# Cross attention of a decoder on one Trainium2 core: half of the score tiles through VectorE with mask and adj added from PSUM, half through ScalarE and GpSimd, and layer norms cut into pieces

## The chip, the cores and the metric

The kernel runs on one core of a Trainium2 chip. A core has five engines that run their own instruction streams and wait for each other by semaphores: TensorE (PE; its weight loads are listed apart as PEld), VectorE (DVE), ScalarE (ACT), GpSimd (POOL) and SyncE (SP), which here issues most DMA transfers. Operands lie in SBUF (128 partitions); matmul results go to PSUM. The metric is the device time of one execution in microseconds; less is better.

## The reference, cut to what matters

The program is a decoder: self-attention, cross attention, two layers of local attention with a feed-forward part, a quantized attention, an attention over media, and a mixture of experts. The stages run one after the other on the same 8 × 512 × 256 array x. The change lies in the cross attention, of B = 8 batches, 512 queries, 512 keys and 16 heads of width 16, all in fp32:

```python
Q = heads(query, Wq, bq)
K = heads(key, Wk, bk)
V = heads(value, Wv, bv)
scores = jnp.einsum('bhqd,bhkd->bhqk', Q, K) / jnp.sqrt(jnp.float32(D))
scores = scores + adj[None, None, :, :]
scores = jnp.where(mask == 0, jnp.float32(-jnp.inf), scores)
weights = jax.nn.softmax(scores, axis=-1)
out = jnp.einsum('bhqk,bhkd->bhqd', weights, V)
out = out.transpose(0, 2, 1, 3).reshape(b, s, E)
return jnp.einsum('bse,ef->bsf', out, Wo.T) + bo
```

A layer norm stands ahead of it (over x, for the queries) and another behind it (for the next stage). The result is added to x.

## The kernel before

**Steps.** The stage is `stage_cross_attention`. Its main loop has 128 steps, 16 for each batch: four groups of four heads (g, e), and for each group four tiles of 128 keys (kt). Scores are held transposed, keys on the partitions and queries along the row, so no maximum over a row is taken; the softmax's sum comes from a column of ones beside the values.

In each step `scores` (L1640) runs four matmuls, one for each head of the group, on four row groups of the array, into two PSUM tiles `sc` of 128 × 2 × 512, two heads in each; three such tiles exist. `soften` (L1657) takes each of the two tiles through ScalarE's exponential into SBUF (`x_e`, six buffers, L1663), and VectorE multiplies it there by `x_share` (L1664), which is exp(adj) where the mask is set and zero elsewhere. `weigh` (L1669) runs two steps behind: four matmuls of the softened tiles with the values, added up over the four key tiles in one PSUM bank `po`.

**After a group.** ScalarE copies `po` to `x_o` (L1685), four DMAs sort its rows into `x_oT` (L1693), the sums go through DRAM into a compact layout, VectorE inverts them (L3174), they come back spread over rows as `x_wide` (L1703), and GpSimd multiplies `x_oT` by `x_wide` (L1696). When both halves of a batch are there, `project_out` (L1709) multiplies by the output weights, VectorE adds the result to x (L1717), the rows are sent to DRAM (`away`, L1720), and the layer norm of the next stage (`lt_ln`) is done on VectorE: statistics, three Newton steps for the inverse root (`rsqrt`, L1460 to L1464, on 128 × 4 elements) and four normalizations (L157).

**Preparing the next batch.** While a batch's steps run, the generator `prepare(b + 1)` gives out pieces of the next batch's preparation: loads (the context, and the mask of 1 MB into `x_mask`, a tile of its own), the layer norm `x_ln`, then `bias` added to x by GpSimd (L1570), two key projections (bias added by VectorE, L1601), four value projections (copied by ScalarE), four pieces of `x_share` (L1560, VectorE, from mask and adj, 128 × 512 each), two transposes and two query projections. All projections, transposes and `project_out` use one PSUM bank, `pj`. `x_share`, keys and queries have one tile for even and one for odd batches.

**What sets the order.** A list `later` of thunks with due steps holds the late parts (inverting, spreading, multiplying, `project_out`), at most two a step. `together` keeps a group's four matmuls adjacent. The framework then schedules the instructions of each engine and adds the waits; within an engine the resulting order is fixed, so an instruction that waits holds up all behind it on that engine. From the twelfth step before the end, the preparation of local attention is mixed in (`ahead.step(3)`), whose rotary embedding is VectorE work.

Of the kernel before, what the change touches and what calls it, by code (L numbers as in the profile page):

```python
# [27 lines left out]
F32 = mybir.dt.float32  # L28
# [11 lines left out]
P = 128  # L40
# [1237 lines left out]
class FastDecoder(Decoder):  # L1278
# [12 lines left out]
    NOWHERE = 8192.0  # L1291

    def __init__(self, ctx, tc, t):
        super().__init__(ctx, tc, t)
        self.sums = self.alloc(self.dram, [self.N_SUMS, 4, S], F32, "sums")
        self.invs = self.alloc(self.dram, [self.N_SUMS, 4, S], F32, "invs")
        self.n_sums = 0
# [158 lines left out]
    def rsqrt(self, pool, out, v, tag):  # L1456
# [4 lines left out]
        for _ in range(3):  # L1461
            nc.vector.scalar_tensor_tensor(t, out, -0.5, out, ALU.mult, ALU.mult)
            nc.vector.tensor_tensor(t, t, v, ALU.mult)
            nc.vector.scalar_tensor_tensor(out, t, 1.5, out, ALU.add, ALU.mult)  # L1464

    def load_cross_attention(self):
        w = self.weights()
        names = "x_wqT", "x_wkT", "b_wvT", "b_woT"
        return [self.load_w(w, 512 * i, self.t[n]) for i, n in enumerate(names)]
# [6 lines left out]
    def stage_cross_attention(self, ahead):  # L1476
# [40 lines left out]
        nc.vector.tensor_tensor(self.ok, self.ok, top, ALU.min)  # L1517
        nc.scalar.activation(adj, adj, AF.Exp)
        for e in range(2):
# [20 lines left out]
        def prepare(b):  # L1540
# [4 lines left out]
            def load():  # L1545
                d["ctxT"] = self.alloc(first, [P, 2, S], F32, "x_ctxT")
                nc.sync.dma_start(
                    d["ctxT"], t["ctxT"].rearrange("(k p) n -> p k n", p=P)[:, :, b * S : (b + 1) * S]
                )
                d["mask"] = self.alloc(first, [P, NST, S], I32, "x_mask", bufs=1)  # L1550
                nc.sync.dma_start(d["mask"], t["x_maskT"][b].rearrange("(k p) q -> p k q", p=P))
                nc.sync.dma_start(
                    self.slots[b * CAP : (b + 1) * CAP, :].rearrange("(p r) c -> p r c", p=P),
                    empty.unsqueeze(1).broadcast_to([P, CAP // P, self.WIDE]),
                )

            def share(k):
                if k == 0:
                    d["share"] = self.alloc(own, [P, NST, S], F32, f"x_share{b % 2}", bufs=1)
                nc.vector.scalar_tensor_tensor(  # L1560
                    d["share"][:, k, :], d["mask"][:, k, :], 0.0, adj[:, k, :], ALU.not_equal, ALU.mult
                )

            def norm():
                x = self.x[:, b * NST : (b + 1) * NST, :]
                stats = self.ln_stats(first, lambda i: [x[:, i, :]], NST, "x_ln")
                d["xn"] = self.alloc(first, [P, NST, C], F32, "x_xn", bufs=1)
                for i in range(NST):
                    self.normalize(d["xn"][:, i, :], x[:, i, :], stats, i)
                nc.gpsimd.tensor_tensor(x, x, bias.unsqueeze(1).broadcast_to([P, NST, C]), ALU.add)  # L1570
                d["xnT"] = self.alloc(first, [P, 2, S], F32, "x_xnT", bufs=1)
# [41 lines left out]

            yield load
            yield norm
            for g in range(2):
                yield lambda g=g: keys(g)
            for i in range(NST):
                yield lambda i=i: values(i)
                yield lambda i=i: share(i)  # L1620
            for c in range(2):
                yield lambda c=c: turn(c)
            for g in range(2):
                yield lambda g=g: queries(g)

        second = None
        for thunk in prepare(0):
            thunk()
            yield
        yield Ahead.MAIN  # L1630

        with self.tc.tile_pool(reuse_waits="tile", name="xa", bufs=2) as pool, self.tc.tile_pool(
# [7 lines left out]
            def scores(n):  # L1640
# [3 lines left out]
                d = held[b]  # L1644
                d.setdefault("e", {})[rest] = pair = []
                for p in range(2):
                    pair.append(self.alloc(psum, [P, 2, 512], F32, "sc", bufs=3))

                for m in self.together(4):
                    r = (m + 2) % 4  # L1650
                    rows = slice(32 * r, 32 * r + 32)
                    nc.tensor.matmul(  # L1652
                        pair[r // 2][:, r % 2, :], d["k"][rows, g, kt * P : (kt + 1) * P], d["q"][rows, e, g, :],
                        start=True, stop=True,
                    )

            def soften(n):  # L1657
                b, rest = divmod(n, 16)
                kt = rest % 4
                d = held[b]  # L1660
                for p in range(2):
                    ex = self.alloc(pool, [P, 2, 512], F32, "x_e", bufs=6)
                    nc.scalar.activation(ex, d["e"][rest][p], AF.Exp)  # L1663
                    nc.vector.tensor_tensor(  # L1664
                        ex, ex, d["share"][:, kt, :].unsqueeze(1).broadcast_to([P, 2, 512]), ALU.mult
                    )
                    d["e"][rest][p] = ex

            def weigh(n):  # L1669
# [7 lines left out]
                for m in self.together(4):  # L1677
                    r = (m + 2) % 4
                    nc.tensor.matmul(  # L1679
                        d["po"][32 * r : 32 * r + 32, :], d["v"][:, kt, 8 * g + 2 * r + e, :],  # L1680
                        ex[r // 2][:, r % 2, :], start=(kt == 0), stop=(kt == 3),
                    )
                if kt == 3:
                    o = self.alloc(pool, [P, S], F32, "x_o", bufs=3)
                    nc.scalar.copy(o, d["po"])  # L1685

                    if e == 0:
                        d["oT", g] = self.alloc(pool, [P, S], F32, "x_oT", bufs=5)
                        d["wide", g] = self.alloc(pool, [P, S], F32, "x_wide")
# [19 lines left out]
            def project_out(b, i):  # L1709
# [6 lines left out]
                x = self.x[:, b * NST + i, :]  # L1716
                nc.vector.tensor_tensor(x, x, ps[:, :C], ALU.add)  # L1717
                if i == NST - 1:
                    rows = self.x[:, b * NST : (b + 1) * NST, :]
                    nc.sync.dma_start(self.away[b], rows)  # L1720
                    stats = self.ln_stats(pool, lambda i: [rows[:, i, :]], NST, "lt_ln")
                    for i in range(NST):
                        self.normalize(rows[:, i, :], rows[:, i, :], stats, i)

            n = 16 * B
            ready = None
            for i in range(n + 2):
                if i < n:
                    if i % 16 == 0:
                        for thunk in ready or ():  # L1730
                            thunk()
                        ready = prepare(i // 16 + 1) if i // 16 + 1 < B else iter(())
                    scores(i)
                    soften(i)
                if i >= 2:
                    weigh(i - 2)

                for _ in range((0, 2, 2, 1, 2, 1, 2)[i % 16] if i % 16 < 7 else 1):
                    thunk = next(ready, None)
                    if thunk is not None:  # L1740
                        thunk()
                later.tick(2)
# [16 lines left out]
    def local_attention(self, l, y, ahead):  # L1759
# [64 lines left out]
        def rotate(d, i):  # L1824
# [13 lines left out]
            q4 = qk.rearrange("p (j h d) -> p j h d", j=2, d=64)  # L1838
            r = self.alloc(first, [P, 2 * S], F32, "la_r")
            r4 = r.rearrange("p (j h d) -> p j h d", j=2, d=64)  # L1840
# [1604 lines left out]
```

## Time and profile before

| | |
|---|---|
| time, median of 3 runs | 3174.21 us (3169.55 to 3178.64) |
| the profiled execution | 3162.05 us |
| its span in the trace | 3160.1 us, mean granted TensorE clock 0.973 |
| cross attention, first score to last weighted sum | 203.4 to about 711 us |
| of these 508 us busy: TensorE / VectorE / ScalarE / GpSimd | 428.4 / 426.4 / 309.2 / 44.8 us |
| mask of 1 MB: issue, landing after issue | 0.4 us, 4.6 to 5.9 us |

A line of the costliest groups gives the line of the code, the engine, the operation, output and inputs by their names in the program, shapes and count; behind the first bar the busy time in all and the mean of one in ns; behind the second the idle time just before them and what ended it. A line of the windows gives a stretch, its length, and busy time and instructions of each engine (PE, PEld, DVE, ACT, POOL), then the granted clock and the share of DMA. A line of the waits reads "who waited <- for what: total us, times, longest". A line of the timeline gives start, length, engine and instruction; in square brackets stands how long its engine had been waiting, and for what.

### The profile page before, as it was taken

What the parts mean: (1) busy time and instruction counts of PE and PEld (TensorE: products, weight loads), DVE (VectorE), ACT (ScalarE), POOL (GpSimd) and SP (SyncE); (2) the same over time, 40 slices, a digit from 0 to 9 for tenths busy, and PEclk for the clock granted to TensorE, in tenths of its full rate; (3) what the DMA queues carried; (4) which work ended last, traced back from release to release, by engine and by line L of the source; (5) the groups of instructions that cost most, each with busy time, mean ns of one, the idle gap of its engine ahead of it and who ended that gap; (6) DMA issues with size and microseconds to landing.
All of it is one profiled execution on the core that took longest, in us unless ns stands there. A gap on an engine that the chain in (4) does not pass through costs nothing. (4 is left out here: it accounts for less than half of the span.)

```text
span 3160.1 us, 40243 instructions
## 1 busy us (share of the span) xinstructions
PE 2877.0 (91%) x14929; PEld 1485.8 (47%) x14944; DVE 2166.9 (69%) x4962; ACT 1154.0 (37%) x1607; POOL 408.7 (13%) x389
## 2 busy tenths in 40 slices
PE   8998888877998989999988989998796999997998
PEld 5642222224555556655555546654444233333665
DVE  7458888887788795357788798558787766566110
ACT  2146556653434431123434431113353444342111
POOL 1111000000011010000101111111201122222111
PEclk9999999989999999999999999999997999998999
DMA  7011111111000001001000011001332122213331
GB/s 237 1 53 44 54 57 48 32 24 51 16 21 22 19 27 42 0 1 35 22 15 21 22 44 61 15 12 60 95 127 94 41 79 103 75 64 103 102 138 59
DMA packets 130695, 168.73 MB, mean 53 GB/s; under 512 B 51760, under 2 KB 79665, under 8 KB 128442
## 3 DMA queue, kind: packets, MB, share of 16 engines
q1 hardware_dynamic: 126394, 154.48, 15.6%
q0 software_dynamic: 4096, 11.59, 1.0%
q8 instruction: 119, 1.95, 0.3%
q14 instruction: 86, 0.70, 0.1%
HBM read 113.12 MB, written 47.50 MB: 51 GB/s over the span
## 5 line engine op out<-in xcount | busy, mean ns | idle before, releaser
L1812 PE MATMUL pj<-w,la_hT 128*128 128x512 f32 x720 | 345.3, 612 | 23.9 <-DVE la_v L1817 21.9
L1664 DVE TENSOR_TENSOR x_e<-x_e,x_share 128x1024 f32<-128x1024 f32 x256 | 309.1, 1253 | 25.1 <-ACT x_e L1663 24.3
L1663 ACT ACTIVATE x_e<-sc 128x1024 f32<-128x1024 f32 x256 | 249.7, 1026 | 147.9 <-PE sc L1652 145.5
L2817 ACT ACTIVATE ma_e<-sc,ma_bias 128x1024 f32<-128x1024 f32 x128 | 142.4, 1114 | 198.8 <-PE sc L2812 185.5
L1812 PEld LDWEIGHTS pj<-w,la_hT 128*128 128x128 f32 x720 | 129.5, 191 | 167.0 <-issue 119.0
L3188 POOL TENSOR_TENSOR la_oT<-la_o,x_wide 128x512 f32<-128x512 f32 x64 | 96.8, 1523 | 790.6 <-DMA x_wide<-invs 654.6
L2825 DVE TENSOR_TENSOR ma_esum<-ma_esum,ma_e 128x1024 f32<-128x1024 f32 x96 | 122.8, 1280 | 91.6 <-ACT ma_e L2817 90.9
L1933 ACT ACTIVATE la_e<-la_e 128x1024 f32<-128x1024 f32 (+1 forms) x128 | 121.4, 951 | 175.2 <-DVE la_e L1929 175.2
L2146 ACT ACTIVATE lf_gate<-pj,lf_b 128x512 f32<-128x512 f32 (+1 forms) x82 | 56.3, 687 | 338.1 <-PE pj L2125 327.1
L1679 PE MATMUL po<-x_e,x_v 128*32 128x512 f32 x1024 | 140.1, 620 | 37.2 <-DVE x_e L1664 34.1
L2125 PE MATMUL pj<-lf_hnT,w 128*128 128x512 f32 (+1 forms) x368 | 171.9, 595 | 1.2 <-DVE lf_hid L2151 1.1
L1929 DVE TENSOR_TENSOR la_e<-sc,la_mask 128x1024 f32<-128x1024 f32 (+1 forms) x128 | 138.3, 1081 | 38.8 <-PE sc L1922 38.8
L1652 PE MATMUL sc<-x_q,x_k 32*128 32x512 f32 x1024 | 159.2, 662 | 0.3 <-ACT x_e L1663 0.2
L2125 PE MATMUL sc<-lf_hnT,w 128*128 128x512 f32 x336 | 158.0, 592 | 0.0
L2197 PE MATMUL po<-w,lf_hid 128*128 128x256 f32 x640 | 148.9, 379 | 0.2 <-DVE x L2207 0.2
L1988 PE MATMUL pj<-w,la_oT 128*128 128x256 f32 x512 | 124.4, 389 | 23.4 <-ACT la_qkT L1858 12.6
L2812 PE MATMUL sc<-ma_qT,ma_kT 64*128 64x512 f32 x512 | 145.2, 644 | 0.0
L2151 DVE SCALAR_TENSOR_TENSOR lf_hid<-sc,lf_b,lf_gate 128x512 f32<-128x512 f32 x70 | 52.4, 748 | 126.3 <-PE sc L2125 126.3
L2835 PE MATMUL po<-ma_e,ma_v 128*64 128x512 f32 x512 | 138.1, 618 | 0.0
L1940 PE MATMUL po<-la_e,la_v 128*64 128x256 f32 (+1 forms) x1024 | 129.1, 374 | 6.4 <-ACT la_o L1962 6.3
L1922 PE MATMUL sc<-la_qkT 64*128 64x256 f32 (+1 forms) x1024 | 132.6, 378 | 1.3 <-DVE la_e L1929 1.3
L1819 ACT ACTIVATE la_sq<-pj 128x512 f32<-128x512 f32 x120 | 71.4, 595 | 156.2 <-PE pj L1812 155.9
(491 smaller groups left out, 5264.5 us busy)
## 6 DMA issues: line engine op xcount, KB each, us to landing
x_wide<-invs SPq DMA_DIRECT2D x184, 128.0 KB
w<-in_f_w_dram SPq DMA_DIRECT2D x16, 1024.0 KB
kv<-kv_o SPq DMA_DIRECT2D x56, 256.0 KB
slots<-x_empty SPq DMA_DIRECT2D x8, 1028.0 KB
x_mask<-in_x_maskT_dram SPq DMA_DIRECT2D x8, 1024.0 KB
ma_kT<-kv SPq DMA_DIRECT2D x8, 1024.0 KB
ma_v<-kv SPq DMA_DIRECT2D x8, 1024.0 KB
ex_rows<-slots SPq DMA_DIRECT2D x7, 1028.0 KB
```

The source lines that it names most:

```text
L1652: nc.tensor.matmul(pair[r // 2][:, r % 2, :], d["k"][rows, g, kt * P : (kt + 1) * P], d["q"][rows, e, g, :], start=True, stop=True,)
L1663: nc.scalar.activation(ex, d["e"][rest][p], AF.Exp)
L1664: nc.vector.tensor_tensor(ex, ex, d["share"][:, kt, :].unsqueeze(1).broadcast_to([P, 2, 512]), ALU.mult)
L1679: nc.tensor.matmul(d["po"][32 * r : 32 * r + 32, :], d["v"][:, kt, 8 * g + 2 * r + e, :], ex[r // 2][:, r % 2, :], start=(kt == 0), stop=( ...
L1812: nc.tensor.matmul(ps, d["hT"][:, k, i * P : (i + 1) * P], wqkv[:, k, j * S : (j + 1) * S], start=(k == 0), stop=(k == 1),)
L1922: nc.tensor.matmul(ps[:, r, jj * 256 : jj * 256 + to - j * P], d["qkT"][rows, 4 + c, j * P : (j + 1) * P], d["qkT"][rows, c, j * P : to], ...
L1929: nc.vector.tensor_tensor(ex[:, :, :n_cols], ps[:, :, :n_cols], mask[:, :n_cols].unsqueeze(1).broadcast_to([P, 2, n_cols]), ALU.add,)
L2125: nc.tensor.matmul(ps[:m, :], w1[:, k, at : at + m], held[b]["hnT"][:, k, :], start=(k == 0), stop=(k == 1))
L2197: nc.tensor.matmul(ps[:, :C], held[b]["hid"][:, f, i * P : (i + 1) * P], w2[:, f, :], start=(f == 0), stop=False,)
L2812: nc.tensor.matmul(ps[:, r, :], d["k"][rows, c, kt * P : (kt + 1) * P], d["q"][rows, c, :], start=True, stop=True,)
L2817: nc.scalar.activation(ex, ps, AF.Exp, bias=bias[:, b * NST + kt : b * NST + kt + 1], scale=0.125)
L2835: nc.tensor.matmul(d["po"][64 * r : 64 * r + 64, :], d["v"][:, kt, 128 * c + 64 * r : 128 * c + 64 * r + 64], ex[:, r, :], start=(kt == 0) ...
```

## The change

The two tiles of a step now belong to different key tiles, in the order of `BLOCKS`: one of the first two (k < 2), one of the last two (k ≥ 2).

- For k < 2 VectorE adds `share` to the scores straight from PSUM into `x_e` (five buffers), and ScalarE takes the exponential in place. For these `share` holds adj, with −BIG where the mask is zero.
- For k ≥ 2 ScalarE takes the exponential from PSUM into `x_ep` (four buffers) and GpSimd multiplies by `share`, which is as before.
- `share` for k < 2 is made by VectorE from the mask and then GpSimd adds adj. The mask is now loaded into the share tile itself and turned into share in place; the tile `x_mask` is gone.
- `weigh` runs three steps behind instead of two.
- The layer norms come in pieces (`ln_pieces`): statistics of each of four rows, a first guess, three Newton steps, four normalizations, each a thunk. `prepare` gives out 13 groups of thunks, one a step; behind `project_out` the pieces are spread over later steps by `later`.
- Buffers: `x_ctxT` 2 to 1, `x_o` 3 to 2, `x_oT` 5 to 4, and `la_r` of local attention 2 to 1.

```diff
+    BLOCKS = (3, 0), (0, 3), (2, 1), (1, 2)
...
+    def ln_pieces(self, pool, rows, out, tag):
+        nc = self.nc
+        mv = self.alloc(pool, [P, NST, 2], F32, tag + "_mv")
+        mean = self.alloc(pool, [P, NST], F32, tag + "_mean")
+        var = self.alloc(pool, [P, NST], F32, tag + "_var")
+        rstd = self.alloc(pool, [P, NST], F32, tag + "_rstd")
+        t = self.alloc(pool, [P, NST], F32, tag + "_t")
+        def stats(i):
+            st = self.alloc(pool, [P, 1, 6], F32, tag + "_bn", bufs=4)
+            nc.vector.bn_stats(st[:, 0, :], rows[:, i, :])
+            nc.vector.bn_aggr(mv[:, i, :], st.rearrange("p a b -> p (a b)"))
+        def guess():
+            nc.vector.tensor_copy(mean, mv[:, :, 0])
+            nc.vector.tensor_scalar(var, mv[:, :, 1], EPS, None, ALU.add)
+            nc.vector.tensor_scalar(
+                rstd.bitcast(I32), var.bitcast(I32), -0.5, float(0x5F3759DF), ALU.mult, ALU.add
+            )
+        def newton():
+            nc.vector.scalar_tensor_tensor(t, rstd, -0.5, rstd, ALU.mult, ALU.mult)
+            nc.vector.tensor_tensor(t, t, var, ALU.mult)
+            nc.vector.scalar_tensor_tensor(rstd, t, 1.5, rstd, ALU.add, ALU.mult)
+        def normal(i):
+            self.normalize(out(i), rows[:, i, :], (mean, rstd), i)
+        return (
+            [lambda i=i: stats(i) for i in range(NST)], [guess] + [newton] * 3,
+            [lambda i=i: normal(i) for i in range(NST)],
+        )
...
-        nc.scalar.activation(adj, adj, AF.Exp)
+        late = adj[:, NST // 2 :, :]
+        nc.scalar.activation(late, late, AF.Exp)
...
-                d["ctxT"] = self.alloc(first, [P, 2, S], F32, "x_ctxT")
+                d["ctxT"] = self.alloc(first, [P, 2, S], F32, "x_ctxT", bufs=1)
...
-                d["mask"] = self.alloc(first, [P, NST, S], I32, "x_mask", bufs=1)
+                d["share"] = self.alloc(own, [P, NST, S], F32, f"x_share{b % 2}", bufs=1)
+                d["mask"] = d["share"].bitcast(I32)
                 nc.sync.dma_start(d["mask"], t["x_maskT"][b].rearrange("(k p) q -> p k q", p=P))
...
-                nc.vector.scalar_tensor_tensor(
-                    d["share"][:, k, :], d["mask"][:, k, :], 0.0, adj[:, k, :], ALU.not_equal, ALU.mult
-                )
...
+                share, mask = d["share"][:, k, :], d["mask"][:, k, :]
+                if k < NST // 2:
+                    nc.vector.tensor_scalar(share, mask, 0.0, -BIG, ALU.is_equal, ALU.mult)
+                    nc.gpsimd.tensor_tensor(share, share, adj[:, k, :], ALU.add)
+                else:
+                    nc.vector.scalar_tensor_tensor(
+                        share, mask, 0.0, adj[:, k, :], ALU.not_equal, ALU.mult
+                    )
...
+            yield [load, rows] + means[:2]
+            yield means[2:]
+            yield [roots[0], roots[1], K[0]]
+            yield [roots[2], K[1]]
+            yield [roots[3], M[0]]
+            yield [normals[0], normals[1], V[0]]
+            yield [normals[2], normals[3], behind]
+            yield [V[1], M[1]]
+            yield [T[0], V[2]]
+            yield [T[1], M[2]]
+            yield [Q[0], V[3]]
+            yield [Q[1]]
+            yield [M[3]]
...
-                for p in range(2):
-                    ex = self.alloc(pool, [P, 2, 512], F32, "x_e", bufs=6)
-                    nc.scalar.activation(ex, d["e"][rest][p], AF.Exp)
-                    nc.vector.tensor_tensor(
-                        ex, ex, d["share"][:, kt, :].unsqueeze(1).broadcast_to([P, 2, 512]), ALU.mult
-                    )
-                    d["e"][rest][p] = ex
+                pair = d["e"][rest]
+                for p in sorted(range(2), key=lambda p: -kts[p]):
+                    share = d["share"][:, kts[p], :].unsqueeze(1).broadcast_to([P, 2, 512])
+                    if kts[p] < NST // 2:
+                        ex = self.alloc(pool, [P, 2, 512], F32, "x_e", bufs=5)
+                        nc.vector.tensor_tensor(ex, pair[p], share, ALU.add)
+                        nc.scalar.activation(ex, ex, AF.Exp)
+                    else:
+                        ex = self.alloc(pool, [P, 2, 512], F32, "x_ep", bufs=4)
+                        nc.scalar.activation(ex, pair[p], AF.Exp)
+                        nc.gpsimd.tensor_tensor(ex, ex, share, ALU.mult)
+                    pair[p] = ex
...
-                    o = self.alloc(pool, [P, S], F32, "x_o", bufs=3)
+                    o = self.alloc(pool, [P, S], F32, "x_o", bufs=2)
...
-                        d["oT", g] = self.alloc(pool, [P, S], F32, "x_oT", bufs=5)
+                        d["oT", g] = self.alloc(pool, [P, S], F32, "x_oT", bufs=4)
...
+                    for k, root in enumerate(roots):
+                        later.add(1 + k, root)
+                    for k, normal in enumerate(normals):
+                        later.add(5 + k // 2, normal)
...
-                if i >= 2:
-                    weigh(i - 2)
...
+                if i >= 3:
+                    weigh(i - 3)
...
-            r = self.alloc(first, [P, 2 * S], F32, "la_r")
+            r = self.alloc(first, [P, 2 * S], F32, "la_r", bufs=1)
```

## The prediction

> **What bounds the kernel now.** I read the page first (busy shares, the 40 slices, the costliest groups), then the windows of the changed stage, batch by batch, then the waits inside it, then single stretches of the timeline. The page's chain of waits covers only a quarter of the span, so I judge the stage by windows and waits.
>
> ```profile
> PE 2877.0 (91%) x14929; PEld 1485.8 (47%) x14944; DVE 2166.9 (69%) x4962; ACT 1154.0 (37%) x1607; POOL 408.7 (13%) x389
> ...
> L1664 DVE TENSOR_TENSOR x_e<-x_e,x_share 128x1024 f32<-128x1024 f32 x256 | 309.1, 1253 | 25.1 <-ACT x_e L1663 24.3
> L1663 ACT ACTIVATE x_e<-sc 128x1024 f32<-128x1024 f32 x256 | 249.7, 1026 | 147.9 <-PE sc L1652 145.5
> ```
>
> TensorE bounds the whole; the two groups below are the change's object. The cross attention runs from 203.4 us (first score) to about 711 us. The windows say us, then busy time of each engine:
>
> ```profile
> 331.00:395.00 64.00, 54.16 (x314) 17.71 (x315) 54.91 (x87) 38.16 (x46) 5.66 (x3) 0.96 0.19 54
> 395.00:459.00 64.00, 55.39 (x320) 18.30 (x318) 53.44 (x86) 38.28 (x46) 4.89 (x3) 0.96 0.18 52
> 203.00:711.00 508.00, 428.37 (x2480) 137.55 (x2478) 426.43 (x651) 309.19 (x375) 44.80 (x26) 0.96 0.15 43
> ```
>
> TensorE and VectorE are equally full (54 of 64), GpSimd nearly empty: neither is at its limit, each waits for the other now and then. The waits between 270 and 650 us (total, times, longest), 6.1 batches at the pitch of 62.5 us between the issues of x_mask:
>
> ```profile
> PEld po L1679 <- DVE x_e L1664: 41.3, 27, 3.6
> PE po L1679 <- DVE x_e L1664: 27.7, 16, 2.8
> PEld pj L1712 <- DVE x L1717: 20.8, 12, 3.8
> PEld pj L1586 <- DVE x_k L1601: 15.2, 6, 3.1
> PE pj L1712 <- DVE x L1717: 10.4, 5, 2.9
> PE pj L1586 <- DVE x_k L1601: 10.1, 5, 2.3
> ```
>
> So TensorE loses 69.0/6.1 = 11.3 us a batch to the multiplied scores and 56.5/6.1 = 9.3 to the one projection bank. Last, how VectorE and GpSimd meet (start, length):
>
> ```profile
> 363.45 0.17 DVE L148 COPY x_ln_mean<-x_ln_mv 128x4 f32<-128x4 f32 x1
> 363.49 2.35 POOL L1570 TENSOR_TENSOR x<-x,x_bias 128x1024 f32<-128x1024 f32 x1 [17.29 <-DVE x_xn L157]
> 363.53 2.35 DVE L1460 TENSOR_SCALAR x_ln_rstd<-x_ln_var 128x4 int32<-128x4 int32 x1
> 365.91 0.16 DVE L1462 SCALAR_TENSOR_TENSOR x_ln_t<-x_ln_rstd 128x4 f32<-128x4 f32 x1
> ```
>
> An operation on 128x4 elements, 0.17 us elsewhere, takes 2.35 us: it ends with GpSimd's.
>
> **What the Trainium skill says.** "SBUF — State Buffer", section "SBUF: two separate sides": VectorE and GpSimd share a port pair as an exclusive lock; who starts first keeps it for the whole instruction, and VectorE needs it in its two-port modes or with two SBUF inputs. The lines above agree, and the reverse is there too: the multiply of x_oT by GpSimd (L1696), 1.27 us alone, took 4.31 us at 653.73 behind three VectorE multiplies. VectorE operations with a PSUM input, and bn_stats, show no such stretch. "VectorE: DVE Perf Modes", section "Why `tensor_tensor` can't do 2×_2P or 4×": an fp32 two-input operation gains nothing from SBUF over PSUM; the trace agrees (PSUM add L1929 1.214 us, SBUF multiply L1664 1.217 median, both 128x1024). "GPSIMD Engine Reference", section "3.1 Elementwise — side-by-side cycle accounting": an add there takes 1.96 times VectorE's; the trace gives 2.35/1.22 = 1.93 (L1570).
>
> **The change, part by part.** All lies in the cross attention; every later stage keeps its order of instructions on each engine.
>
> *VectorE* loses 16 of 32 multiplies a batch, and its 16 others become PSUM adds: 53.4 − 32×1.253 + 16×1.214 = 33 us a batch. *ScalarE* keeps 32 exponentials, half from SBUF (1.058 us, L1933) instead of PSUM (1.026): 39 us, no change. *GpSimd* gets 16 multiplies at 2.35 (the row L1570, same shape) = 37.6, two adds of adj on 128x512 at 1.27 (row L1696) = 2.5, beside its old 2.35 + 2×1.27: 45 us a batch of about 62. It stays below the pitch, with 17 us to spare.
>
> *TensorE* does the same work. From start-to-start pitches of groups that follow each other without a wait (scores 1.07, weighted sums 0.99, keys and queries 1.9, values and output projection 1.06, transposes 1.1): 16×1.07 + 16×0.99 + 4×1.9 + 8×1.06 + 2×1.1 = 51.3 us a batch. The 11.3 us of waiting for multiplied scores should go: weigh now lags three steps, and the slowest way (exponential 1.03, multiply 2.35) is shorter than one step pair. The 9.3 us for the projection bank waits on VectorE's queue, which drops from 53 to 33 us; I take half, 4.7. Base pitch: 56 us, 6.5 below now; 8×56 = 448.
>
> *The lock.* Of VectorE's operations in a batch, 36 small ones (L157, L1460 to L1464 and their like in the pieces, mask to share) need the pair; they fill 9.5 us together and each may wait for a 2.35 us multiply. The 16 big adds read PSUM and don't. In a batch's middle VectorE has 20 us spare, so this costs nothing there; at a boundary it does, below. The pieces don't stay apart: the scheduler puts 8 Newton operations behind one add and 12 behind another.
>
> *The mask*, which has no case in the old trace. Before, it had a tile of its own, was issued a batch ahead, and nobody waited for it. Now it lands in the share tile, which batch b−1 reads until its last VectorE add and last GpSimd multiply. In the new order the changed kernel's L1601 (mask to share for b+1) is VectorE's next instruction after the first add of batch b; behind it stand all further adds, and on GpSimd the two adds of adj stand between the first and second multiply. On SP the waiting issue holds back a group's sums and the last group's copies, which are wanted a dozen steps later: nothing. Before the mask can be read: release by the last multiply, issue 0.4 and 1 MB of landing, 4.6 to 5.9 us after issue (207.71 and later issues): 5.2. Then two L1601 (0.7 each, as the old L1560's 0.68) alternating with two GpSimd adds (1.27) and two new L1604 (0.68), partly side by side: 4.5. Then the adds of steps 1 and 2, which the scores of step 3 need for their PSUM: 2.4. Sum 12.1 us after the last multiply. TensorE has meanwhile the last weighted sum (0.99), K0 (1.9) and part of step 2: 3.4. Loss: 8.7 us. It occurs at batches 1 to 6 (batch 0 prepares into a fresh tile, batch 7 prepares nothing). At 2 to 6 two normalizations (0.35 each) of the batch before stand ahead of it and can meet one multiply (2.35): 3 more, 11.7. Bounds of one boundary: 7 (spare work of TensorE fits better) and 12.
>
> *The rest*: la_r with one buffer is used by VectorE alone, nothing. x_o and x_oT with one buffer less: a batch makes four and two, released long before, nothing. Fill and the longer lag at the end: 2 us. In the last batch local attention's rotary work (VectorE, two SBUF inputs, about 7 us a cluster) alternates with the multiplies: 0 to 8, I take 4.
>
> Sum: 448 + 8.7 + 5×11.7 + 2 + 4 = 521 against 508: 13 us more. The span is 3160.1, with 2 around it, so 3162.05 becomes 3175. This execution lies 12 below the median of 3174.21; I shift the median: **3187 us**. A change below 0.3% (9.5 us) can't be told from none.
>
> **Rivals.** The break-even is (508 − 448 − 6)/6 = 9.0 us a boundary: under it the change is faster.
>
> *1: the boundaries are mild.* 7 us each, base pitch 54.5 (little of the bank's wait left): 436 + 42 + about 0 = 478, 30 less: 3145. For it: before, TensorE often runs a step ahead, and the spare work can cover the landing. Against it: adds behind L1601 are strictly in order, and three pairs of score banks hold no more than that. Decided by whether VectorE's second add of a batch starts less than 9 us after the last multiply.
>
> *2: the boundary is hidden and TensorE's floor rules.* 8×52 + 6×4 + 4 = 444, 64 less: 3110. It needs the transfer to be nearly covered, which no buffer allows; for it speaks only the 11.3 us of removed waiting.
>
> *3: GpSimd is the bound.* 45 us, plus all 9.5 of the locking operations, plus a boundary in which it waits for the mask and the two adds (about 10), plus handovers (16 × 0.35): 70 us a batch, 8×70 − 508 = +52 and some 4 for the end: 3230. For it: the 4.31 us multiply, and "Perfetto Trace Analysis", section "GPSIMD Engine Instruction", warns that GpSimd's spans are unreliable, so 2.35 can be off (no run here tells yet; start to start they fit). Against it: 17 us of room.
>
> **How the numbers follow.** Forecast 0.45 (own range 3165 to 3212), rival 1 0.25, rival 2 0.12, rival 3 0.18. The range runs from between rivals 1 and 2 to rival 3, 3128 to 3232, leaving about a tenth on each side. Faster: rival 2 whole, 0.21 of rival 1, 0.05 of the forecast's lower end = 0.38. Within 0.3%: 0.13 + 0.04 = 0.17. Slower: 0.27 + 0.18 = 0.45.
>
> **What would show it.** Right: x_share's transfer named as what L1601 waits for, six times, 3 to 6 us each; TensorE idle 7 to 12 us at each boundary; no weighted sum waiting on VectorE or GpSimd between boundaries; VectorE about 33 us busy a batch, GpSimd 45. Wrong: waits for x_ep spread over the batch (rival 3), or a pitch below 60 us in batches 1 to 6 (rivals 1, 2). If GpSimd's multiply is not near 2.35 us, or VectorE's PSUM adds are stretched by it, the sum falls.

## The result and the profile after

The changed kernel takes 3279.7 us (median of 4 runs, 3275.84 to 3280.04) against 3172.3 us before (median of 4 runs): a ratio of 1.033, 95% interval 1.0315 to 1.0351. The forecast was 3187, the range ended at 3232.

The page of the changed kernel, busy shares and the groups of the changed part:

```profile
PE 2959.2 (90%) x14944; PEld 1507.0 (46%) x14944; DVE 2089.2 (64%) x4834; ACT 1153.6 (35%) x1607; POOL 729.2 (22%) x533
...
L1726 POOL TENSOR_TENSOR x_ep<-x_ep,x_share 128x1024 f32<-128x1024 f32 x128 | 304.0, 2390 | 232.4 <-ACT x_ep L1725 232.2
...
L1722 ACT ACTIVATE x_e<-x_e 128x1024 f32<-128x1024 f32 x128 | 135.4, 1058 | 271.3 <-DVE x_e L1721 270.7
L1721 DVE TENSOR_TENSOR x_e<-sc,x_share 128x1024 f32<-128x1024 f32 x128 | 155.0, 1216 | 103.7 <-PE sc L1706 102.8
```

The durations are what the forecast used: the add 1.216 us (forecast 1.214), the exponential from SBUF 1.058 (1.058), GpSimd's multiply 2.36 in the median (2.35). What is new is the idle time behind the bars: ScalarE waits 271 us for VectorE's adds, GpSimd 232 us for ScalarE. Before, nearly all that ScalarE waited for was scores (145.5 of 147.9 us at L1663). The waits between 270 and 700 us, total, times, longest:

```profile
ACT x_e L1722 <- DVE x_e L1721: 184.8, 56, 9.9
POOL x_ep L1726 <- ACT x_ep L1725: 158.2, 46, 8.0
...
PEld sc L1706 <- DVE x_e L1721: 65.2, 47, 6.7
...
DVE x_inv L3236 <- DMA x_sums<-sums: 49.1, 15, 7.3
...
PE sc L1706 <- DVE x_e L1721: 34.8, 14, 5.8
...
DVE x_share L1601 <- DMA x_share<-in_x_maskT_dram: 25.3, 6, 7.5
...
PE po L1739 <- ACT x_o L1746: 19.9, 18, 1.4
...
PE pj L1651 <- ACT x_q L1639: 12.6, 5, 2.7
...
PE pj L1651 <- ACT x_xnT L1626: 7.4, 6, 1.3
```

Weight loads (PEld) overlap matmuls (PE), and one stall can show in both, so the two are not added here. The matmuls themselves stood idle 34.8 us for adds, before they might write scores, and 39.9 us for ScalarE's copies, before they might use the bank of the weighted sums or the projection bank. The two windows over batches 1 to 6 (first before, then after; the last numbers are the granted TensorE clock, the share of DMA and GB/s) show VectorE and GpSimd both far from full after the change, and TensorE granted less than before:

```profile
260.00:629.00 369.00, 316.51 (x1880) 105.16 (x1880) 308.49 (x464) 229.04 (x277) 31.57 (x17) 0.98 0.17 48
...
274.00:719.00 445.00, 369.33 (x1872) 116.12 (x1868) 241.80 (x372) 229.05 (x276) 273.36 (x126) 0.88 0.15 43
```

Of the 76 us by which the second window is longer, only 23 are more idle time of the matmuls (52.5 to 75.7 us). The other 53 are more busy time for almost the same number of instructions, at a clock of 0.88 instead of 0.98. The ends of matmuls are modelled, so this split is rough. The Trainium skill, "TensorE: Matmul & The Clock Gate", section "Part 1: The HAM clock gate (the "warmup" mystery)", says that an idle array falls to half its clock and needs some busy time to come back; the trace agrees: four matmuls for the keys took 3.78 us at 371.05, after the gaps of a boundary, and four of the same shape for the queries 1.98 at 319.90:

```profile
319.90 1.98 PE L1631 MATMUL pj<-x_xnT,w 128*128 128x512 f32 x4
...
371.05 3.78 PE L1631 MATMUL pj<-x_ctxT,w 128*128 128x512 f32 x4
```

Where the time went, batch by batch, from the first scores of a batch to the first of the next (the last batch to its last weighted sum), in one profiled execution of each kernel:

| batch | before | forecast | after |
|---|---|---|---|
| 0 | 56.8 | 56 | 69.5 |
| 1 to 6, sum | 368.4 | 403.2 | 445.4 |
| 7 | 82.3 | 62 | 101.4 |

And step by step in batches 1 to 6, mean us from scores to scores:

| step | 0 | 1 | 2 | 3 | 4 | 5 | 6 | 7 | 8 | 9 | 10 | 11 | 12 | 13 | 14 | 15 |
|---|---|---|---|---|---|---|---|---|---|---|---|---|---|---|---|---|
| before | 2.2 | 4.5 | 5.9 | 5.8 | 4.2 | 2.1 | 3.7 | 3.1 | 2.1 | 3.3 | 2.7 | 4.0 | 6.6 | 5.0 | 4.2 | 2.1 |
| after | 5.3 | 5.1 | 6.5 | 8.1 | 2.1 | 4.8 | 2.1 | 5.0 | 2.7 | 5.0 | 4.0 | 10.2 | 3.1 | 4.2 | 3.1 | 2.9 |

Two places stand out: the boundary (steps 0 to 3, 25.0 us), and step 11 (11.9 to 13.3 us in batches 0 to 3, 6.3 to 9.4 in batches 4 to 6). The boundary between batches 1 and 2 in VectorE's timeline (start, length):

```profile
346.85 2.36 DVE L1493 SCALAR_TENSOR_TENSOR lt_ln_t<-lt_ln_rstd 128x4 f32<-128x4 f32 x1
349.24 2.27 DVE L1494 TENSOR_TENSOR lt_ln_t<-lt_ln_t,lt_ln_var 128x4 f32<-128x4 f32 x1
...
352.99 1.22 DVE L1721 TENSOR_TENSOR x_e<-sc,x_share 128x1024 f32<-128x1024 f32 x1
...
354.76 1.22 DVE L1721 TENSOR_TENSOR x_e<-sc,x_share 128x1024 f32<-128x1024 f32 x1
359.44 1.59 DVE L1601 TENSOR_SCALAR x_share<-x_share 128x512 f32<-128x512 int32 x2 [3.46 <-DMA x_share<-in_x_maskT_dram]
360.96 0.24 DVE L3236 RECIPROCAL x_inv<-x_sums 128x16 f32<-128x16 f32 x1
361.12 3.27 DVE L1604 SCALAR_TENSOR_TENSOR x_share<-x_share,x_adj 128x512 f32<-128x512 int32 x2
364.31 2.34 DVE L1721 TENSOR_TENSOR x_e<-sc,x_share 128x1024 f32<-128x1024 f32 x2
```

Two Newton operations of 0.16 us take 2.3 us each beside GpSimd, so the last add of the batch comes at 353.0; it lets the mask's transfer go (issued at 354.27), and the second add of the new batch comes at 364.31, with L1604 held by GpSimd too (1.6 us each instead of 0.68). That is the boundary which the forecast described. TensorE's matmuls were busy 19.0 of its 25.2 us, at a mean clock of 0.76:

```profile
348.30:373.50 25.20, 19.00 (x75) 4.87 (x72) 16.56 (x21) 9.31 (x10) 16.06 (x8) 0.76 0.18 58
```

Step 11 of batch 1, in the timeline of all engines:

```profile
317.94 2.60 DVE L157 TENSOR_SCALAR x_xn<-x,x_ln_mean,x_ln_rstd 128x256 f32<-128x256 f32 x4 [1.91 <-PE pj L1623]
...
320.62 2.35 POOL L1612 TENSOR_TENSOR x<-x,x_bias 128x1024 f32<-128x1024 f32 x1 [1.20 <-DVE x_xn L157]
320.66 2.34 DVE L1488 TENSOR_SCALAR x_ln_rstd<-x_ln_var 128x4 int32<-128x4 int32 x1
...
323.27 1.19 DVE L1721 TENSOR_TENSOR x_e<-sc,x_share 128x1024 f32<-128x1024 f32 x1
...
324.49 1.06 ACT L1722 ACTIVATE x_e<-x_e 128x1024 f32<-128x1024 f32 x1 [5.97 <-DVE x_e L1721]
...
326.83 1.46 ACT L1639 ACTIVATE x_q<-pj,x_qb,x_qsc 128x512 f32<-128x512 f32 x2
...
328.34 2.07 PE L1651 MATMUL pj<-w,x_ctxT 128*128 128x256 f32 x4 [2.70 <-ACT x_q L1639]
...
332.21 2.82 PE L1631 MATMUL pj<-x_xnT,w 128*128 128x512 f32 x4
334.40 0.25 DVE L3236 RECIPROCAL x_inv<-x_sums 128x16 f32<-128x16 f32 x1 [7.29 <-DMA x_sums<-sums]
334.96 1.14 PE L1706 MATMUL sc<-x_q,x_k 32*128 32x512 f32 x8
```

Five microseconds of small VectorE work stand ahead of the add at 323.27; the guess (L1488), 0.17 us elsewhere, takes 2.34 beside GpSimd's operation at 320.62. ScalarE is stuck for 5.97 us with the exponential of that add; the copy of the queries stands behind it, so the projection bank stays taken; TensorE waits 2.70 us, comes back at half speed (2.07 us for four matmuls that take 1.13 at 315.19), and the next scores start at 334.96, 13 us after those of step 11. The reciprocal's wait of 7.29 us looks worst, but with the reciprocal moved, alone, the step stays as long (below).

### The profile page after: what moved, and what is told of

It reads as the page before. It is cut to its first block, busy times and chain, and to the rows that moved or that the text cites. A ratio compares the mean times of both kernels' runs of the same rounds, so it can differ in the third digit from the quotient of the medians.

```text
span 3274.1 us, 40264 instructions
## 1 busy us (share of the span) xinstructions
PE 2959.2 (90%) x14944; PEld 1507.0 (46%) x14944; DVE 2089.2 (64%) x4834; ACT 1153.6 (35%) x1607; POOL 729.2 (22%) x533
## 5 line engine op out<-in xcount | busy, mean ns | idle before, releaser
L1726 POOL TENSOR_TENSOR x_ep<-x_ep,x_share 128x1024 f32<-128x1024 f32 x128 | 304.0, 2390 | 232.4 <-ACT x_ep L1725 232.2
L1706 PE MATMUL sc<-x_q,x_k 32*128 32x512 f32 x1024 | 196.6, 692 | 50.5 <-DVE x_e L1721 49.5
L1722 ACT ACTIVATE x_e<-x_e 128x1024 f32<-128x1024 f32 x128 | 135.4, 1058 | 271.3 <-DVE x_e L1721 270.7
L1721 DVE TENSOR_TENSOR x_e<-sc,x_share 128x1024 f32<-128x1024 f32 x128 | 155.0, 1216 | 103.7 <-PE sc L1706 102.8
L1739 PE MATMUL po<-x_e,x_v 128*32 128x512 f32 x512 | 153.5, 683 | 23.3 <-ACT x_o L1746 23.3
L1739 PE MATMUL po<-x_ep,x_v 128*32 128x512 f32 x512 | 153.5, 683 | 0.0
L2050 PE MATMUL pj<-w,la_oT 128*128 128x256 f32 x512 | 125.1, 391 | 24.1 <-DVE x L2055 10.8
```

Source lines behind the costliest of these rows:

```text
L1706: nc.tensor.matmul(pair[r // 2][:, r % 2, :], d["k"][rows, g, kts[r // 2] * P : (kts[r // 2] + 1) * P], d["q"][rows, e, g, :], start=True, ...
L1721: nc.vector.tensor_tensor(ex, pair[p], share, ALU.add)
L1722: nc.scalar.activation(ex, ex, AF.Exp)
L1726: nc.gpsimd.tensor_tensor(ex, ex, share, ALU.mult)
L1739: nc.tensor.matmul(d["po"][32 * r : 32 * r + 32, :], d["v"][:, self.BLOCKS[kt][r // 2], 8 * g + 2 * r + e, :], ex[r // 2][:, r % 2, :], st ...
```

## The experiments

Each time is a median, each ratio is to the kernel before as it ran beside it, with its 95% interval; lengths of steps come from one profiled execution of each run; differences between runs are taken from the ratios, times 3172 us. The changed kernel's ratio is 1.0333. First, the buffer of the context, which the forecast had not spoken of, and the place of the mask's work. "Tied" means that an instruction is ordered on VectorE behind the add of the step in which the code gives it out.

**Two buffers for the context.**

```diff
-                d["ctxT"] = self.alloc(first, [P, 2, S], F32, "x_ctxT", bufs=1)
+                d["ctxT"] = self.alloc(first, [P, 2, S], F32, "x_ctxT", bufs=2)
```

> The changed kernel with two buffers for x_ctxT again. Theory A (one buffer: the transfer of the next context waits on SyncE for the last value projection, the sums of a group queue behind it, the reciprocal that needs them holds all later adds on VectorE): the step that follows the third group, 10.2 us long in batches 1 to 6 and 13.3 in batch 0 of the changed kernel, falls to the 3.5 us of its neighbours. 6 x 6.7 + 9.8 = 50 us less: about 3230 us. Theory B (the stage is slow because GpSimd and VectorE take turns at the shared port, whatever the buffers): within 10 us of 3280. Theory C (the mask's wait alone): within 10 us of 3280.

Measured: 3281.8, ratio 1.0344 (1.0316 to 1.0372). Nothing, and step 11 stayed at 10.2 us. The theory fell: the sums have to reach DRAM before they can be read back, and the transfer of the context is issued in that time. With two buffers it is even issued at the same place, for a batch later.

**The mask's work tied.**

```diff
+        return self.tc.issue_after(self.added) if self.added is not None else ExitStack()
...
-                    nc.vector.tensor_scalar(share, mask, 0.0, -BIG, ALU.is_equal, ALU.mult)
+                    with self.after_add():
+                        nc.vector.tensor_scalar(share, mask, 0.0, -BIG, ALU.is_equal, ALU.mult)
```

> The changed kernel with the four makings of x_share tied behind the adds of steps 4, 7, 9 and 12, where the code gives them out, instead of right behind the first add of a batch. Theory C (VectorE waits for the mask there): the first four steps of a batch, 25.0 us in batches 1 to 6, lose the wait for the transfer (25.3 us in all by the trace) and the alternation with GpSimd behind it (some 4 a batch), about 45 to 50 us less; but the sums of the third group still queue on SyncE behind the mask's issue, which may give 2 to 3 us a batch back, so 25 to 50 less: 3230 to 3255. Theories A and B: within 10 us of 3280.

Measured: 3251.4, ratio 1.0247 (1.0220 to 1.0274): 27 us less. This lies in the range of theory C. The mask's wait is gone from the list, but the reciprocal's grew from 49 to 89 us (270 to 700 us again):

```profile
DVE x_inv L3245 <- DMA x_sums<-sums: 89.2, 24, 7.5
```

The steps 2 and 3 fell from 14.6 to 10.0 us; steps 0 and 1, where the lock has delayed the last add of the batch before, stayed.

**Both edits together.**

> Both edits. If A and C are both right and lie in different places of the batch, their gains add up: 75 to 100 us less than the changed kernel, 3180 to 3205, level with the kernel before or 1% above it. If the one takes the other's place (B), much less than the sum.

Measured: 3250.8, ratio 1.0244 (1.0220 to 1.0269), the mask's gain alone, since theory A was wrong.

**The pieces tied too.**

```diff
         def newton():
+          with self.after_add():
             nc.vector.scalar_tensor_tensor(t, rstd, -0.5, rstd, ALU.mult, ALU.mult)
```

(and the same for the guess and the normalizations)

> As the run before, and the guess, each Newton step and each normalization tied behind the add of the step in which the code gives them out, so that the pieces stand apart. If the cluster of 12 small operations behind one add, each of which can wait for a 2.35 us multiply of GpSimd, delays the batch's last add (5 us between 346.8 and 352 us in the trace of the changed kernel): 4 to 5 us a batch, 20 to 30 us less than the run before. If VectorE has the room: within 10 us of it.

Measured: 3238.6, ratio 1.0208 (1.0183 to 1.0233): 11 us less by the medians, between the two theories, and the intervals overlap. Step 0 fell from 5.3 to 2.1 and step 11 from 11.1 to 6.3, but steps 3, 5 and 7, where the pieces stand now, grew by 1.4, 1.3 and 2.0.

**The reciprocal tied, alone and with all the rest.**

```diff
         def invert():
-            nc.vector.reciprocal(inv, small)
+            with self.after_add():
+                nc.vector.reciprocal(inv, small)
```

> The changed kernel with nothing but the reciprocal of the sums (the cross attention's only) tied behind the add of the step in which the code gives it out: in the order it moves from behind the first, fourth, ninth and twelfth add of a batch to behind the second, sixth, tenth and fifteenth. Theory D (VectorE now stands ahead of ScalarE, so a wait of VectorE for a DMA keeps PSUM from coming free; the scheduler puts the reciprocals right behind adds, 49 us of waits for x_sums between 270 and 700 us): the long step after the third group (10.2 and 13.3 us) falls to 6.3, the length of the step in the run with all pieces tied; 6 x 4 + 7 = 31 us, with the other reciprocals 30 to 50 less: 3230 to 3250. If the reciprocal's wait only covers another wait (the one for the projection bank): within 10 us of 3280.

> All ties together: two buffers for x_ctxT, share, pieces and reciprocals in the steps in which the code gives them out. Theory D: the 62 us of waits for x_sums that the run without the last tie had between 270 and 675 us go for the most part, 20 to 45 us less than its 3238.6: 3195 to 3220. If what is left there is the shared port: within 10 us of 3238.

Measured: alone 3274.7, ratio 1.0327 (1.0291 to 1.0364); with all the rest 3242.0, 1.0230 (1.0200 to 1.0260). Nothing in both places: the longest named wait of VectorE covered other waits.

**No multiplies on GpSimd.**

```diff
-                        nc.gpsimd.tensor_tensor(ex, ex, share, ALU.mult)
+                        nc.vector.tensor_tensor(ex, ex, share, ALU.mult)
```

> The run before with the multiply of the second tile on VectorE instead of GpSimd: no lock, but VectorE has 16 more operations of 1.22 us in a batch (53 us instead of 33), and each stands in the queue ahead of an add. Theory of the port (the small operations of VectorE lose some 8 us a batch to GpSimd's multiplies): 20 to 40 us less than the run before. Theory of the queue (what matters is what stands ahead of an add on VectorE): 10 to 40 us more than the run before.

Measured: 3227.8, ratio 1.0193 (1.0158 to 1.0227): 12 us less than with GpSimd. The gain lies below the first theory's range, and the second expected a loss: without GpSimd's multiplies, and with their work on VectorE, the net gain is small.

**ScalarE's order.** In the changed kernel the exponentials of two VectorE tiles come first, then those of two PSUM tiles. ScalarE's own timeline shows it (x_e is the VectorE tile, x_ep the PSUM tile):

```profile
386.39 1.07 ACT L1722 ACTIVATE x_e<-x_e 128x1024 f32<-128x1024 f32 x1
387.80 0.39 ACT L1655 COPY x_v<-pj 128x256 f32<-128x256 f32 x1 [0.35 <-PE pj L1651]
390.20 1.06 ACT L1722 ACTIVATE x_e<-x_e 128x1024 f32<-128x1024 f32 x1 [2.01 <-DVE x_e L1721]
391.16 1.01 ACT L1725 ACTIVATE x_ep<-sc 128x1024 f32<-128x1024 f32 x1
392.06 0.58 ACT L1626 COPY x_xnT<-pj 128x512 f32<-128x512 f32 x1
392.53 1.04 ACT L1725 ACTIVATE x_ep<-sc 128x1024 f32<-128x1024 f32 x1
```

The scores of the first PSUM tile wait in their bank until the *next* step's scores are through VectorE, and so does a copy that frees the projection bank. The edit:

```diff
-                        nc.scalar.activation(ex, ex, AF.Exp)
+                        with self.tc.issue_after(first_exp):
+                            nc.scalar.activation(ex, ex, AF.Exp)
                     else:
                         ex = self.alloc(pool, [P, 2, 512], F32, "x_ep", bufs=4)
                         nc.scalar.activation(ex, pair[p], AF.Exp)
+                        first_exp = self.nc.cur_bb.bb.instructions[-1]
```

With all ties:

> All ties, and on ScalarE the exponential of a step's PSUM tile always ahead of that of its VectorE tile (in the changed kernel the order is e, e, p, p over two steps, so that the first PSUM tile's exponential waits for the add of the next step). Theory E (this order keeps two PSUM tiles occupied while ScalarE waits for VectorE; 151 us of such waits between 270 and 675 us): 15 to 40 us less than without this edit. If PSUM comes free by the adds alone: within 10 us of it.

Measured: 3194.5, ratio 1.0087 (1.0055 to 1.0120), 45 us less than with all ties alone, somewhat more than theory E gave. And as the only edit; in the cross attention the orders of TensorE and VectorE are unchanged, and GpSimd's but for two swapped places:

> The changed kernel with one edit: on ScalarE the exponential of a step's PSUM tile ahead of that of its VectorE tile; the orders of TensorE and VectorE stay, and so do the mask's wait, the bunched pieces and the early reciprocals. Theory E (the ring scores - add - exponential of the added tile - exponentials of two PSUM tiles - next scores sets the pace of every pair of steps): 45 to 70 us less than 3280, 3210 to 3235. Theory F (the order helps only when the other waits are gone): 0 to 20 less, 3260 to 3280.

Measured: 3241.0, ratio 1.0206 (1.0173 to 1.0238), 40 us less, slightly under what theory E gave and far from F. This is the largest gain of a single edit. It is spread: in batches 1 to 6 steps 2, 5, 7, 9, 11 and 15 each fell by 0.8 to 1.0 us, and step 11 is still 9.3 us. The timeline of ScalarE with all ties and this order:

```profile
382.51 1.06 ACT L1735 ACTIVATE x_e<-x_e 128x1024 f32<-128x1024 f32 x1 [0.85 <-DVE x_e L1732]
383.47 1.01 ACT L1738 ACTIVATE x_ep<-sc 128x1024 f32<-128x1024 f32 x1
385.72 1.06 ACT L1735 ACTIVATE x_e<-x_e 128x1024 f32<-128x1024 f32 x1 [1.25 <-DVE x_e L1732]
386.68 1.01 ACT L1738 ACTIVATE x_ep<-sc 128x1024 f32<-128x1024 f32 x1
```

ScalarE still waits for adds, but for one at a time, with nothing of an older step behind it.

**One step later still**, the VectorE tile's exponential behind the PSUM tile of the next step:

```diff
-                        nc.scalar.activation(ex, ex, AF.Exp)
+                        waiting.append(ex)
                     else:
                         ex = self.alloc(pool, [P, 2, 512], F32, "x_ep", bufs=4)
                         nc.scalar.activation(ex, pair[p], AF.Exp)
+                        flush()
```

> All ties, and the exponential of the VectorE tile one step later still, behind the PSUM tile of the next step, so that ScalarE hardly ever waits for an add. Theory E: the 71 us of waits of ScalarE for VectorE that the run with the PSUM tile first had between 270 and 640 us shrink, 5 to 20 us less than its 3194.5. If what is left comes from late adds on VectorE and the projection bank: within 8 us of 3194.5.

Measured: 3199.1, ratio 1.0084 (1.0059 to 1.0109): no further gain, as the second alternative had it.

**The last batch without GpSimd's multiplies.**

```diff
+                        eng = nc.vector if b == B - 1 else nc.gpsimd
+                        eng.tensor_tensor(ex, ex, share, ALU.mult)
```

> All ties, the PSUM tile first, and in the last batch alone the second tile multiplied by VectorE instead of GpSimd. From the start of the last batch to the first score of local attention the kernel before takes 114 us, the run without this edit 128. If the rotary work of local attention (two SBUF inputs) loses this to GpSimd's multiplies at the shared port: 5 to 12 us less than 3194.5. If it is VectorE's queue: none, or 5 more.

Measured: 3193.7, ratio 1.0071 (1.0045 to 1.0097). In the trace the stretch from the last batch's start to local attention's first score is 123.9 us instead of 128.3, but the time is within the intervals of the run without the edit: inconclusive.

**The longer lag alone, in the kernel before.**

```diff
-                    ex = self.alloc(pool, [P, 2, 512], F32, "x_e", bufs=6)
+                    ex = self.alloc(pool, [P, 2, 512], F32, "x_e", bufs=8)
...
-                if i >= 2:
-                    weigh(i - 2)
+                if i >= 3:
+                    weigh(i - 3)
```

> The kernel before with one part of the change alone: the weighted sums three steps behind the scores instead of two (x_e with eight buffers instead of six; room from x_ctxT and la_r with one buffer and x_oT with four). If the 69 us of waits for multiplied scores that the kernel before had between 270 and 650 us are real losses, the lag takes up to 11 us a batch away: 3100 to 3150. If VectorE's 53.5 us a batch or the projection bank take over at once: 3160 to 3180.

Measured: 3180.6, ratio 1.0029 (1.0020 to 1.0038), a touch slower. The matmuls' waits for multiplied scores fell from 27.7 to 1.4 us, and as much came back at the next thing that needs VectorE, the keys' bank (270 to 650 us; before 15.2 and 10.1):

```profile
PEld pj L1586 <- DVE x_k L1601: 41.3, 6, 6.9
PE pj L1586 <- DVE x_k L1601: 36.3, 6, 6.1
...
PE po L1679 <- DVE x_e L1664: 1.4, 6, 0.2
```

So what TensorE waited there was not to be had by a longer lag: VectorE, busy about 53 us of each batch of 61, was only waited for elsewhere.

**All ties, ScalarE's order, no GpSimd** (the edits of these runs together).

> All ties, the PSUM tile first on ScalarE, and the second tile multiplied by VectorE everywhere: the change without GpSimd's multiplies and so without the lock. If the 24 us by which the run with GpSimd (3194.5) still lies above the kernel before come from the port and from GpSimd's 2.36 us: 10 to 25 us less than it, 3170 to 3185. If they come from adds that stand behind other work on VectorE: 0 to 25 more, 3195 to 3220.

Measured: 3183.4, ratio 1.0033 (1.0021 to 1.0046), 17 us less than with GpSimd, of the 28 that were left. This counts the port, GpSimd's slower multiply and the added work of VectorE together. This is the best form of the change found, still 0.3% above the kernel before.

**The pieces tied alone** (the edit of the fourth run on the changed kernel).

> The changed kernel with the pieces of the layer norms alone tied behind the adds of their steps; the mask's wait, the reciprocals and ScalarE's order stay. Theory G (the long step after the third group, 10 to 13 us, comes from four normalizations and a root that stand together behind the tenth add and wait 2.4 us each for GpSimd's operations; the late add holds ScalarE, ScalarE holds the projection bank, TensorE stands still and comes back at half its clock): that step falls to 6.3 us and the first step of a batch from 6 to 2.1, 6 x (4 + 3.5) + 7 = 50 us, of which a part is lost again where the pieces stand now: 25 to 45 us less than 3280. If the pieces' place doesn't matter: within 10 us of 3280.

Measured: 3264.1, ratio 1.0290 (1.0272 to 1.0308), 14 us less, under the range of theory G and over that of its rival. Step 11 fell to 6.3 in batches 0 to 6 and step 0 to 2.1, both exactly as theory G had them, so the bunch of pieces is the cause of that long step. That GpSimd stretches the bunch is seen in the timeline and has no run of its own. But most of it came back: step 7 grew from 5.0 to 9.0, and steps 2 and 3 from 14.6 to 17.4.

**The three gaining edits without the two idle ones** (ScalarE's order, share and pieces tied).

> The three edits that gained something (the PSUM tile first on ScalarE, pieces and share tied) without the two that gained nothing (second buffer of x_ctxT, reciprocals tied). If those two are worth nothing beside the others either: within 8 us of 3194.5. If the reciprocals matter once ScalarE's order is right: 10 to 25 us more.

Measured: 3217.2, ratio 1.0149 (1.0125 to 1.0173), 20 us more than with the other two. With ScalarE's order right, one of the two is worth 20 us after all, most likely the reciprocals: step 3, behind a reciprocal, is 10.4 us here and 7.0 with them tied. What each edit is worth depends on which others are in, since each seems to uncover the next wait in VectorE's queue.

## Why the prediction was wrong

*Durations, GpSimd's load, transfer, lock.* Right: 1.216, 1.058 and 2.36 us; GpSimd at 273/6 = 45.6 us a batch (forecast 45); the mask named as L1601's wait six times, 25.3 us in all (3.5 to 3.7 us five times, but 7.5 once; forecast 3 to 6 each); adds from PSUM never stretched (1.227 us at most). Rival 3 did not come true: GpSimd is not the bound, it waits for ScalarE. VectorE is busy 40.3 us a batch, not 33. In the best form of the change, without GpSimd's multiplies, it is 52.4, and 32.9 without the 16 multiplies that came back to it; so some 7 us a batch (an estimate, 40.3 less 32.9) are time in which VectorE's operations wait for GpSimd and count as busy. The forecast's 33 left that out.

*The boundary.* Right in size, in part by luck: steps 0 to 3 take 25.0 us. The quiet steps (4 to 10 and 12 to 15) average 39.0/11 = 3.5 us, so four of them would be 14.2: a loss of 10.8, forecast 8.7 to 11.7. But the forecast took 8.7 of it from the mask, and the run with the mask's work tied takes away only 4.6 us a batch in steps 2 and 3. The Newton steps ahead of the last add are another part, as steps 0 and 1 show when they are tied (5.3 to 2.1 and 5.1 to 4.4 us). And TensorE did not idle 7 to 12 us there: its matmuls idled 6.2 us in the boundary shown above, and much of the rest is slower work.

*"In a batch's middle VectorE has 20 us spare, so this costs nothing there."* This step failed first, and with it the one that gave ScalarE "39 us, no change". The spare time is there (242 of 445 us busy) and does not help. ScalarE takes its work in order, and in the new kernel half of its exponentials wait for an add. A late add so holds ScalarE, with it the second tile's scores, the copy of the weighted sums and the projection bank, and with these TensorE, which comes back at half its clock. Batches 1 to 6 miss the forecast by 42 us. ScalarE's order put right, alone, takes 31 us off them (445.4 to 414.7; 40 us of the whole time), spread over the steps. The bunch of small VectorE operations is a second cause: it makes step 11 long. That step lies 6.7 us above the quiet steps in the mean of batches 1 to 6, and tying the pieces alone took 3.9 of these away; ScalarE's order alone took 1.0. As the tied pieces cost time elsewhere, these batches gained only 10 us by it. The gains overlap and are not to be added. The forecast followed TensorE's and VectorE's orders for what each instruction waits for, and counted ScalarE by its busy time alone.

*The last batch.* The sum took 56 + 6 us for it, because 8 × 56 treats all batches alike. In the old trace it took 82.3 us, with local attention's preparation mixed in, and the windows showed it: 48.7 us of TensorE in the last 64. After the change it is 101.4. Of the 39 us missed here, 20 are this wrong base; the other 19 came with the new order. In the traces the last batch takes 93.5 us with all ties and ScalarE's order, and 88.0 without GpSimd's multiplies as well. What share of this the port has, or the rotary work ahead of adds, stays open: in the time, the run with VectorE's multiplies in the last batch could not tell.

*Batch 0.* Forecast 56, because its mask goes to a fresh tile; it took 69.5: 13.3 us in step 11 and 16.4 in steps 2 and 3. A fresh tile does not help there. The makings of share for batch 1 stand behind the first add all the same, start at 209.25, 4.9 us after the mask's issue at 204.33 (such a transfer landed 4.6 to 5.9 us after issue before the change), and take 7.3 us beside GpSimd, so that the second add comes at 216.51. (The trace names an exponential as the end of the wait at 209.25, whose result this operation does not read; the landing itself was not singled out.)

```profile
206.00 1.21 DVE L1721 TENSOR_TENSOR x_e<-sc,x_share 128x1024 f32<-128x1024 f32 x1
209.25 2.92 DVE L1601 TENSOR_SCALAR x_share<-x_share 128x512 f32<-128x512 int32 x2 [2.04 <-ACT x_ep L1725]
212.09 4.50 DVE L1604 SCALAR_TENSOR_TENSOR x_share<-x_share,x_adj 128x512 f32<-128x512 int32 x2
216.51 2.34 DVE L1721 TENSOR_TENSOR x_e<-sc,x_share 128x1024 f32<-128x1024 f32 x2
```

With them tied, steps 2 and 3 of batch 0 take 9.5 us.

*"The 11.3 us of waiting for multiplied scores should go."* The figure adds the waits of weight loads (41.3) and of matmuls (27.7), which in part are the same stalls; the matmuls alone lost 27.7/6.1 = 4.5 us a batch. In the same way the 9.3 us for the projection bank are too many: with 51.3 us of work, 11.3 and 9.3 would make 71.9, not 62.5. The waits went: between 270 and 700 us of the changed kernel no matmul stands idle for a multiplied tile, and the weight loads waited 5.1 us for GpSimd. But the lag alone brought nothing in the kernel before. And even the best form of the change has batches of 62.6 us (1 to 6), not the 56 of the base pitch: what takes the rest, after the lock, the mask and the orders are out, was not isolated.

The misses add up: 13.5 + 42 + 39 = 95 us in the stage, against 3279.7 − 3187 = 93 in the time. The break-even of 9.0 us a boundary could not hold either, because it was drawn from that base.

## What to carry to other kernels

Before moving work from one engine to another, write down for each in-order engine what every instruction waits for in the new order, also where the engine is far from full: here ScalarE, 229 of 445 us busy, passed each delay of VectorE on to TensorE. Spare time of an engine helps only where no other engine in the loop waits for it. Take the base of a sum from each stretch by itself, above all the last one, where the next stage is mixed in. And before adding up waits, see whether they are the same stall seen twice.

## What was unexpected of the hardware

TensorE's granted clock in batches 1 to 6 fell from 0.98 to 0.88, and half speed showed after gaps as short as 2.7 us (four matmuls at 328.34 in 2.07 us instead of 1.13, the four for the queries behind them in 2.82 instead of 1.98), which makes the work behind each stall slower. No run separated this from the stalls themselves; with all ties, ScalarE's order and no GpSimd the clock was back at 0.98, TensorE's busy time in batches 1 to 6 was 337.6 us (316.5 before, 369.3 in the changed kernel), and the kernel was still not faster than before.
